# Last stage of a four-layer graph network: a new static order of its steps on the engines

## The chip, the core and the metric

The kernel runs on one core of a Trainium2 chip. The core has five engines that work side by side, each through its own queue in order: TensorE for matmuls (PE; its weight loads are the row PEld), VectorE (DVE), ScalarE (ACT), GpSimd (POOL), and SyncE (SP), which here only issues DMAs. An engine whose next instruction has to wait does nothing else until that wait ends. The metric is the device time of one execution in microseconds (us).

## The reference, cut to what matters

128 graphs of 128 nodes with 128 features pass through four layers; each layer adds its result to `x`. Layers 2 and 3 (counted from 0) are attention layers, and with the end of layer 1 they make up the stage that the change touches.

```python
h = relu(layernorm(x)); x = x + L0(h, adj)      # relations, normalised
h = relu(layernorm(x)); x = x + L1(h, adj)      # pairwise |x_i - x_j| scores, batch norms over all graphs
h = relu(layernorm(x)); x = x + L2(h, adj)      # 4 heads:
    h = (x @ W + b).reshape(B, N, 4, 32)
    e = leaky(e_i[:, :, None] + e_j[:, None, :]);  e = where(adj > 0, e, NEG)
    out = einsum('bijh,bjhd->bihd', softmax(e, axis=2), h)
h = relu(layernorm(x)); x = x + L3(h, adj)      # 1 head, then elu
```

`L1` ends with a batch norm over all graphs, so nothing after it can start before every graph has passed through the pairwise part.

## The kernel before

Graphs are taken in 32 groups of four (`G = 4`, `NG = 32`). The kernel has three stages, one after the other: layer 0 with the pairwise products of layer 1 (lines 264 to 712), the scores and softmax of layer 1 (714 to 1111), and the last stage (1308 to 1570), which does the end of layer 1 and the whole of layers 2 and 3. A fourth path (`last_stage`, 1122) is taken only for inputs out of bounds and doesn't run here.

In the last stage `attention(g)` (line 1319) writes down the work of one group as up to 59 steps. A step has a name, an engine, a cost in us, the steps that it comes after, the PSUM tiles that it takes and gives back, and the function that emits its instructions. In order of dependence one group is:

- `lz`, `lx` (SP): loads of the layer-1 result and of `x`; five groups have both on the chip and need none. `off` (POOL): the mask. `y` (ACT), `yl` (DVE), `po` (PE), `x1` (DVE): end of layer 1.
- layer 2: `mv2` (DVE, moments), `rs2` (POOL, root, lines 228, 229, 1386, 1387), `h2` (ACT, four instructions, line 1392), `pt2` (PE, transposes), `hT2` (ACT), `pr2` (PE, projection), `v2` (DVE), `w12` (POOL, fill), `wr2` (ACT), `sp2` (POOL, the scores split into three bf16 pieces), `pe2` (PE), `left2` (ACT), `right2` (DVE). Then for the four graphs `ps0`, `ps2` (PE, scores of two graphs each), `e0` to `e3` (ACT, two exponentials each, lines 1481 and 1482), `e0m` to `e3m` (DVE), `w0` to `w3` (PE), `o1`, `o3` (DVE, division by the sums), and `x2` (DVE).
- layer 3: the same chain with one head, `mv3`, `rs3`, `h3`, `pt3`, `hT3`, `pr3`, `v3`, `w13`, `wr3` (line 1433), `sp3`, `pe3`, `left3`, `right3`, `ps`, `e`, `em`, `pv` (line 1544), `o` (line 1549), then `ex` (ACT, line 1558), `x3`, `x4` (DVE), and `out` (SP, line 1563).

That is 15 steps on ACT (28 instructions), 15 on PE, 19 on DVE, 7 on POOL, and up to 3 DMAs for each group.

`_planned` (line 78) turns the steps of all groups into one sequence. It is a list scheduler: it keeps the time at which each engine comes free, and repeatedly takes the step that can start earliest. Group number n may not start before `(n - FIRST) * PERIOD`, that is every 12 us from the sixth on. It counts the PSUM tiles (`ONE = 4` single banks, `TWO = 2` double banks) but not the SBUF buffers of `BUFS` (12 for `x`, 6 for `y`, 2 or 3 for most others); those are waited for on the chip, by the instruction that needs the buffer. Its costs are written into the steps, for instance `h` 1.2, `y` 0.75, `pr` 1.0, `w0` 0.95, `e` 1.05. The sequence fixes the order of every engine's queue; when a step starts on the chip is decided by the semaphores.

`split` (1435) writes into one of four `pieces` buffers, chosen by `g % 4`. Earlier stages use another scheduler, `_ordered` (113).

Of the kernel before, what the change touches and what calls it, by code (L numbers as in the profile page):

```python
# [14 lines left out]
OP = mybir.AluOpType  # L15
# [20 lines left out]


ONE, TWO = 4, 2
PERIOD, FIRST, HOP, LANDING = 12, 5, 0.2, 3.0
HOP1 = 0.4  # L40
TINY = 2.0 ** -100
BUFS = {"y": 6, "x": 12, "off": 10, "st": 8, "mv2": 3, "rs2": 3, "nb2": 3, "h": 7, "hT2": 3, "v2": 3, "wr2": 7,
        "left2": 5, "right2": 5, "e0": 2, "e1": 2, "e2": 2, "e3": 2, "sums2": 3, "o2": 2, "mv3": 2, "rs3": 2,
        "nb3": 2, "hT3": 2, "v3": 2, "wr3": 3, "left3": 2, "right3": 2, "e": 2, "sums3": 3, "o3": 3, "ex": 3}


def _bcast(src, n):
# [17 lines left out]
def _staggered(works, gap):  # L65

    flying, turn = [], 0
    while True:
# [4 lines left out]
                return  # L73
        turn += 1
        flying = [w for w in flying if next(w, works) is not works]


def _planned(groups, period, banks):

    free, done = dict.fromkeys(("SP", "Pool", "ACT", "DVE", "PE"), 0.0), {}
    left = {tag: [0.0] * n for tag, n in banks.items()}
    tag = lambda name: "2" if name[0] == "2" else "1"
    waiting = [list(steps) for steps in groups]
    plan = []
    while any(waiting):
        best = None
        for n, steps in enumerate(waiting):
            for i, (name, engine, cost, after, takes, last, work) in enumerate(steps):  # L90
                if any(a not in done for a in after):
                    continue
                start = max([free[engine], (n - FIRST) * period] + [done[a] + HOP for a in after])
                if takes:
                    bank = sorted(left[tag(takes[0])])
                    if len(bank) < len(takes):
                        continue
                    start = max(start, bank[len(takes) - 1])
                if best is None or start < best[0]:
                    best = start, n, i  # L100
        start, n, i = best
        name, engine, cost, after, takes, last, work = waiting[n].pop(i)
        free[engine] = start + cost
        done[name] = start + cost + (LANDING if engine == "SP" else 0)
        for one in takes:
            left[tag(one)].remove(min(left[tag(one)]))
        for one in last:
            left[tag(one)].append(start + cost + HOP)
        plan.append((start, len(plan), work))
    return [work for _, _, work in sorted(plan, key=lambda p: p[:2])]  # L110


def _ordered(steps, limits, hop):
# [21 lines left out]
    while len(plan) < len(steps):  # L135
        best = None
        for engine, names in ready.items():
            could = []
            for name, since in names.items():
                takes = named[name][4]  # L140
                if all(left[tag] for tag in takes):
                    could.append((max([free[engine], since] + [min(left[tag]) for tag in takes]),
                                  named[name][6], name))
            if could:
                first = min(could)[0]
                one = min((c for c in could if c[0] == first), key=lambda c: c[1])
                if best is None or first < best[0]:
                    best = one
        start, _, name = best
        _, engine, cost, _, takes, gives, _, work = named[name]  # L150
        del ready[engine][name]
        free[engine] = start + cost
        done[name] = start + cost + (LANDING if engine == "SP" else 0)
        for tag in takes:
            left[tag].remove(min(left[tag]))
        for tag in gives:
            left[tag].append(start + cost + hop)
        plan.append(work)
        for f in followers.get(name, ()):
            missing[f] -= 1  # L160
            if missing[f] == 0:
                released(f)
    return plan


@with_exitstack
def tile_gnn_stack(ctx: ExitStack, tc: tile.TileContext, a: dict, out: bass.AP):
# [1140 lines left out]
    with tc.If(nc.values_load(bounded, min_val=0, max_val=1) > 0) as cmp, \  # L1308
# [7 lines left out]
                nc.gpsimd.memset(one, 1.0)  # L1316
                pieces[heads].append(one)

        def attention(g):


            t, steps = {}, []

            def step(name, engine, cost, after, work, takes=(), last=()):
                steps.append(((g, name), engine, cost, [(g, n) for n in after], takes, last, work))

            def sb(name, shape, dtype=F32):
                t[name] = p3.tile(shape, dtype, tag=name, bufs=BUFS[name], name=name)
# [23 lines left out]
            def masked():  # L1352
                nc.gpsimd.tensor_scalar(sb("off", [P, G, P], BF16), M8[g], 0.0, None, op0=OP.is_equal)

            step("off", "Pool", 1.5, lx, masked)
            step("y", "ACT", 0.75, () if on_chip else ("lz",), lambda: nc.scalar.activation(
                t["y"], t["y"], AF.Identity, bias=bias2, scale=scale2[:, 0:1]))
            step("yl", "DVE", 0.65, ("y",), lambda: nc.vector.scalar_tensor_tensor(
                t["y"], t["y"], 0.01, t["y"], op0=OP.mult, op1=OP.max))

            def rest():
                po = bank("po")
                for k in range(G):
                    nc.tensor.matmul(po[:, k, :], t["y"][:, k, :], wtyT, start=True, stop=True)

            step("po", "PE", 0.9, ("yl",), rest, takes=("po",))
            step("x1", "DVE", 0.6, ("po",) + lx, lambda: nc.vector.tensor_tensor(t["x"], t["x"], t["po"], OP.add),
                 last=("po",))

            def layer(n, heads, wx, first):  # L1370
# [62 lines left out]
                            nc.scalar.copy(wr[:, 2 * a:2 * a + 2, 0:P], pr[:, a, :, 0:P])  # L1433

                def split():
                    v, to = t[q("v")], pieces[heads][g % len(pieces[heads])]
                    t[q("sides")] = to
                    for p in range(3):

# [18 lines left out]
                def right():  # L1458
# [1 line left out]
                                            t[q("pe")][0:rows, 1:2, :].to_broadcast([rows, 4, P]),  # L1460
                                            own[0:rows, :, None].to_broadcast([rows, 4, P]), OP.mult)

                step(mv, "DVE", 1.05, ("x1",) if first else ("x2",), moments)
                step(rs, "Pool", 1.7, (mv,), root)
                step(q("h"), "ACT", 1.2, (rs,), normed)
                step(q("pt"), "PE", 0.5, (q("h"),), turned, takes=(q("pt"),))
                step(q("hT"), "ACT", 0.52, (q("pt"),), lambda: nc.scalar.copy(sb(q("hT"), [P, G, P]), t[q("pt")]),
                     last=(q("pt"),))
                step(q("pr"), "PE", 1.0, (q("hT"),), projected, takes=("2" + q("pr"),))
                step(q("v"), "DVE", 0.3, (q("pr"),), scores)  # L1470
                step(q("w1"), "Pool", 0.3, (q("h"),), values)
                step(q("wr"), "ACT", 0.65, (q("v"), q("w1")), values2, last=("2" + q("pr"),))
                step(q("sp"), "Pool", 1.2, (q("v"),), split)
                step(q("pe"), "PE", 0.2, (q("sp"),), crossed, takes=(q("pe"),))
                step(q("left"), "ACT", 0.3, (q("pe"),), lambda: nc.scalar.copy(
                    sb(q("left"), [P, P], BF16)[0:rows], t[q("pe")][0:rows, 0, :]))
                step(q("right"), "DVE", 0.6, (q("left"),), right, last=(q("pe"),))

            def exps(ps, e):

# [7 lines left out]
            for k in range(G):  # L1488
# [20 lines left out]
                                         start=True, stop=True)  # L1509

                if k % 2 == 0:
                    step(ps, "PE", 0.8, ("right2", "off"), summed, takes=(ps, f"ps{k + 1}"))
                step(e, "ACT", 1.05, (f"ps{k // 2 * 2}",), lambda ps=ps, e=e: exps(ps, e))
                step(e + "m", "DVE", 0.62, (e,), lambda ps=ps, e=e: higher(ps, e), last=(ps,))
                step(f"w{k}", "PE", 0.95, (e + "m", "wr2") + ((f"w{k - 1}",) if k % 2 else ()), weighed,
                     takes=("2" + pv,) if k % 2 == 0 else ())
                if k % 2:
                    def scaled(k=k, pv=pv):
# [4 lines left out]
                        nc.vector.tensor_tensor(t["o2"][:, k - 1:k + 1, :].rearrange("p k (a b) -> p k a b", a=4),  # L1523
                                                t[pv][:, :, :, 0:32], sums.to_broadcast([P, 2, 4, 32]), OP.mult)

                    step(f"o{k}", "DVE", 0.55, (f"w{k}",) + (("o1",) if k == 3 else ()), scaled, last=("2" + pv,))

            step("x2", "DVE", 0.62, ("o3",), lambda: nc.vector.scalar_tensor_tensor(
                t["x"], t["o2"], -1.0, t["x"], op0=OP.add, op1=OP.add))

            layer(3, 1, w3x, False)
# [14 lines left out]
            def scaled3():  # L1546
# [2 lines left out]
                nc.vector.tensor_tensor(sb("o3", [P, G, P]).rearrange("p (a b) c -> p a b c", a=2),  # L1549
                                        t["pv"][:, :, :, 0:P], sums.to_broadcast([P, 2, 2, P]), OP.mult)  # L1550

            step("ps", "PE", 0.7, ("right3",), summed3, takes=("ps",))
            step("e", "ACT", 1.05, ("ps",), lambda: exps("ps", "e"))
            step("em", "DVE", 0.62, ("e",), lambda: higher("ps", "e"), last=("ps",))
            step("pv", "PE", 1.0, ("em", "wr3"), weighed3, takes=("2pv",))
            step("o", "DVE", 0.75, ("pv",), scaled3, last=("2pv",))

            step("ex", "ACT", 0.52, ("o",), lambda: nc.scalar.activation(sb("ex", [P, G, P]), t["o3"], AF.Exp))
            step("x3", "DVE", 0.62, ("o",), lambda: nc.vector.scalar_tensor_tensor(
                t["x"], t["o3"], 0.0, t["x"], op0=OP.max, op1=OP.add))  # L1560
            step("x4", "DVE", 0.62, ("x3", "ex"), lambda: nc.vector.scalar_tensor_tensor(
                t["x"], t["ex"], 1.0, t["x"], op0=OP.min, op1=OP.add))
            step("out", "SP", 0.4, ("x4",), lambda: nc.sync.dma_start(
                out[g * G:g * G + G].rearrange("b t c -> t b c"), t["x"]))
            return steps

        with tc.manual_schedule():
            groups = [attention(g) for g in sorted(range(NG), key=lambda g: g not in Y)]
            for work in _planned(groups, PERIOD, {"1": ONE, "2": TWO}):
                work()  # L1570


# [40 lines left out]
```

## Time and profile before

| | |
|---|---|
| median of 3 runs | 2754.09 us (2749.94 to 2755.46) |
| the profiled execution's own time | 2756.67 us |
| its span, first to last instruction | 2754.8 us |
| busy over the span: PE, DVE, ACT, POOL | 89%, 90%, 86%, 62% |
| first instruction of the last stage that uses the batch norm (`y` on ACT) | at 2291.34 us |
| last instruction of the last stage on DVE (`x4`) | starts at 2748.94 us |
| last `out` issued, issue to landing | at 2749.7 us, 2.4 us |
| mean granted TensorE clock | 0.974 |

The profile is of one execution. Its rows give, for an engine and a line of the kernel, how many instructions ran, how long one took, and what ended the idle time in front of it. The view by stretches gives busy time of each engine between two moments; the count in brackets is instructions.

### The profile page before, as it was taken

What the parts mean: (1) busy time and instruction counts of PE and PEld (TensorE: products, weight loads), DVE (VectorE), ACT (ScalarE), POOL (GpSimd) and SP (SyncE); (2) the same over time, 40 slices, a digit from 0 to 9 for tenths busy, and PEclk for the clock granted to TensorE, in tenths of its full rate; (3) what the DMA queues carried; (4) which work ended last, traced back from release to release, by engine and by line L of the source; (5) the groups of instructions that cost most, each with busy time, mean ns of one, the idle gap of its engine ahead of it and who ended that gap; (6) DMA issues with size and microseconds to landing.
All of it is one profiled execution on the core that took longest, in us unless ns stands there. A gap on an engine that the chain in (4) does not pass through costs nothing.

```text
span 2754.8 us, 41902 instructions
## 1 busy us (share of the span) xinstructions
PE 2450.1 (89%) x14521; PEld 1183.4 (43%) x14521; DVE 2477.0 (90%) x4738; ACT 2378.7 (86%) x2821; POOL 1699.9 (62%) x1628
## 2 busy tenths in 40 slices
PE   6999999999999999999997888988888987999896
PEld 3333333333333333333332343444444445777775
DVE  6999999999999999999998799888888887899876
ACT  5999999999999999999998777788877866899885
POOL 6999999999999999999985010010011115565642
PEclk8999999999999999999999999999999999999998
DMA  3455555555555555555542999999999971112200
GB/s 113 180 206 201 206 203 204 205 200 203 199 203 199 203 199 203 202 199 208 200 200 92 408 409 395 386 410 410 411 410 407 409 271 35 56 61 66 62 20 25
DMA packets 185426, 611.43 MB, mean 222 GB/s; under 512 B 31987, under 2 KB 99702, under 8 KB 121718
## 3 DMA queue, kind: packets, MB, share of 16 engines
q1 hardware_dynamic: 184768, 608.50, 57.4%
q8 instruction: 118, 1.93, 0.3%
q14 instruction: 102, 0.84, 0.1%
q10 hardware_dynamic: 438, 0.17, 0.0%
HBM read 312.58 MB, written 296.03 MB: 221 GB/s over the span
## 4 chain that ended last, share of the span: by engine, by line
ACT 34%; PE 22%; DVE 19%; issue 11%; DMA 8%; POOL 5%; SPq 0%; ACTq 0%; POOLq 0%; DVEq 0%
ACT d L365 11%; ACT z L341 11%; PE ps L814 5%; PE hp L327 5%; DVE z L857 4%; DVE d L317 3%; DMA z<-hp 3%; DMA rows<-sk 3%; PE hp L330 2%; POOL d L317 2%; PE pk L821 2%; DMA u<-rows 2%; ACT h L1392 2%; ACT o L462 2%; ACT h L503 2%
## 5 line engine op out<-in xcount | busy, mean ns | idle before, releaser
L317 POOL TENSOR_TENSOR d<-xe 128x2048 f32<-128x2048 f32 x256 | 1074.3, 4202 | 68.6 <-PE hp L327 51.3
L327 PE MATMUL hp<-d,w1T 128*64 128x512 f32 x4096 | 997.3, 601 | 105.5 <-ACT z L341 87.9
L365 ACT ACTIVATE d<-d 128x2048 f32<-128x2048 f32 x384 | 735.6, 1936 | 9.5 <-POOL d L317 5.7
L317 DVE TENSOR_TENSOR d<-xe,xp 128x2048 f32<-128x2048 f32 x256 | 579.0, 2262 | 7.2 <-PE hp L327 4.2
L327 PEld LDWEIGHTS hp<-d,w1T 128*64 128x64 f32 x4096 | 286.6, 136 | 621.0 <-issue 463.4
L341 ACT COPY z<-hp 128x1024 f32<-128x1024 f32 x512 | 517.2, 1029 | 37.1 <-PE hp L330 33.9
L905 POOL TENSOR_TENSOR x<-x,bt 128x512 f32<-128x512 f32 x32 | 50.1, 1565 | 669.0 <-DMA x<-x 540.5
L355 DVE BATCH_NORM_STATS2 st<-z 128x6 f32<-128x512 f32 x512 | 348.9, 682 | 43.4 <-ACT z L341 43.2
L356 DVE BATCH_NORM_STATS2 st<-z 128x6 f32<-128x512 f32 (+1 forms) x512 | 328.9, 642 | 0.0
L857 DVE SCALAR_TENSOR_TENSOR z<-z 128x2048 f32<-128x2048 f32 x128 | 299.4, 2339 | 7.9 <-ACT z L839 7.9
L839 ACT ACTIVATE z<-z,bias,scale 128x2048 f32<-128x2048 f32 x128 | 267.1, 2087 | 10.1 <-DVE bias L751 7.9
L843 ACT ACTIVATE zr<-z,bias,scale 128x2048 f32<-128x2048 f32 x128 | 267.3, 2088 | 0.9 <-DMA z<-hp 0.9
L330 PE MATMUL hp<-both_t,xw 128*64 128x512 f32 x1024 | 267.8, 594 | 0.0
L814 PE MATMUL ps<-z,w2z 128*32 128x512 f32 x1024 | 142.6, 629 | 61.2 <-DVE z L857 60.5
L821 PEld LDWEIGHTS pk<-pick,su 128*128 128x128 f32 x1024 | 125.8, 193 | 145.6 <-DVE su L835 107.1
L821 PE MATMUL pk<-pick,su 128*128 128x16 f32 x1024 | 138.3, 267 | 31.6 <-DVE su L835 31.0
L1508 PE MATMUL pv<-wr,e 128*128 128x128 f32 x1024 | 140.3, 283 | 5.8 <-DVE e L1485 4.0
L330 PEld LDWEIGHTS hp<-both_t,xw 128*64 128x64 f32 x1024 | 81.3, 138 | 140.0 <-issue 140.0
L814 PE MATMUL ps<-zr,w2r 128*32 128x512 f32 x1024 | 140.3, 620 | 0.0
L814 PE MATMUL ps<-z,w2l 128*32 128x512 f32 x1024 | 139.6, 614 | 0.0
L1508 PEld LDWEIGHTS pv<-wr,e 128*128 128x128 f32 x1024 | 128.3, 196 | 13.7 <-DVE e L1485 4.4
L1485 DVE SCALAR_TENSOR_TENSOR e<-e,ps 128x512 f32<-128x512 f32 x160 | 106.5, 676 | 26.6 <-ACT ps L1482 25.8
(241 smaller groups left out, 3798.0 us busy)
## 6 DMA issues: line engine op xcount, KB each, us to landing
hp<-z SPq DMA_DIRECT2D x248, 1024.0 KB, 3.9
z<-hp SPq DMA_DIRECT2D x248, 1024.0 KB, 13.2
x<-x SPq DMA_DIRECT2D x118, 256.0 KB, 6.0
u<-rows SPq DMA_DIRECT2D x32, 384.0 KB, 11.6
x<-in_x_dram SPq DMA_DIRECT2D x32, 256.0 KB, 5.6
adj<-in_adj_dram SPq DMA_DIRECT2D x32, 256.0 KB, 5.8
out_dram<-x SPq DMA_DIRECT2D x32, 256.0 KB, 2.4
z<-y SPq DMA_DIRECT2D x27, 256.0 KB, 11.9
```

The source lines that it names most:

```text
L317: eng.tensor_tensor(d, ahead, x[:, None, None, :].to_broadcast([P, 2, KC, P]), OP.max if t == BY_MAX else OP.subtract)
L327: nc.tensor.matmul(hp[64 * hh:64 * hh + 64, c:c + 512], w1T2 if by_max else w1T, d[:, hh, c:c + 512], start=True, stop=not by_max, skip_gr ...
L330: nc.tensor.matmul(hp[64 * hh:64 * hh + 64, c:c + 512], XW[i // NT // 2][:, i // NT % 2, :], both_t.rearrange("p h k i -> p h (k i)")[:, h ...
L341: nc.scalar.copy(half_of(b, t), linear.pop(i))
L355: nc.vector.bn_stats(st[:, 2 * t, :], hs[:, 0:512])
L356: nc.vector.bn_stats(st[:, 2 * t + 1, :], hs[:, 512:1024 - P * last])
L365: nc.scalar.activation(diffs[i], diffs[i], AF.Abs)
L814: nc.tensor.matmul(ps[32 * c:32 * c + 32, :], w[:, w0:w0 + 32], v[:, 512 * c:512 * c + 512], start=j0 == 0, stop=w is w2r, skip_group_chec ...
L821: nc.tensor.matmul(pk[:, kk, 0:16], su[:, kk, :], pick.rearrange("p h j -> p (h j)"), start=True, stop=True)
L843: nc.scalar.activation(zr, z1, AF.Relu, bias=bias1, scale=scale1[:, 0:1])
L857: nc.vector.scalar_tensor_tensor(z0, z0, 0.01, z0, op0=OP.mult, op1=OP.max)
L1508: nc.tensor.matmul(t[pv][:, k % 2, hd, :], t[e][:, hd, :], flat[:, at:at + P], start=True, stop=True)
```

## The change

`_planned` is replaced by `_ranked`, and the steps get new costs, ranks and joining times. No instruction is added, removed or altered; the index of the `pieces` buffer changes from the group's number to its place in the turn.

```diff
-PERIOD, FIRST, HOP, LANDING = 12, 5, 0.2, 3.0
+LANDING = 3.0
 HOP1 = 0.4
+HOPS, DEEP, ARRIVING, NEAR = 0.1, 0.25, 2.4, 0.025
+LATE = {"SP": 0.0, "Pool": 0.02, "ACT": 0.1, "DVE": 0.08, "PE": 0.1}
+LANDED = {"load": 6.0, "out": 5.0, "out0": 5.0}
+TILES = (("y", "lz", "po"), ("x", "lx", "out"), ("off", "off", "ps0 ps2 ps"), ("mv2", "mv2", "rs2"), ("rs2", "rs2", "h2"),
...
+EVERY = 16.7
+RANK3 = {"off": 260, "y": 228, "yl": 425, "po": 78, "x1": -85, "mv2": 311, "rs2": 127, "h2": 106, "pt2": -67,
...
+         "pv": -160, "o": -8, "ex": 360, "x3": 119, "x4": 187, "out": 299, "lz": 146, "lx": -73}
+JOIN3 = (20, 2, 0, 0, 1, 2, 28, 29, 0, 13, 49, 23, 67, 94, 51, 151,
+         131, 78, 137, 199, 221, 127, 166, 143, 241, 183, 223, 276, 237, 165, 178, 294)
-def _planned(groups, period, banks):
...
+def _ranked(steps, limits, held, hop, within=0.0):
+    named, place = {q[0]: q for q in steps}, {q[0]: n for n, q in enumerate(steps)}
+    free, done, left = dict.fromkeys(LATE, 0.0), {}, {tag: [0.0] * n for tag, n in limits.items()}
+    needs, reads, open_ = {}, {}, []
+    for tag, at, readers in held:
+        if at in named:
+            of = needs.setdefault(at, {})
+            of[tag] = of.get(tag, 0) + 1
+            for r in readers:
+                reads.setdefault(r, []).append(len(open_))
+            open_.append([tag, len(readers), 0.0])
...
+    while len(plan) < len(steps):
+        best = None
+        for engine, names in ready.items():
+            could = []
+            for name in names:
+                start = max(free[engine], since[name])
+                for tag, n in needs.get(name, {}).items():
+                    start = max(start, sorted(left[tag])[n - 1] if len(left[tag]) >= n else 1e9)
+                could.append((start, named[name][4], place[name], name))
+            if could and (best is None or min(could)[0] < best[0]):
+                first = min(could)[0]
+                best = (first,) + min((c for c in could if c[0] <= first + within), key=lambda c: c[1:3])
...
+        free[engine], done[name] = round(start + cost - LATE[engine], 2), round(start + cost, 2)
+        if engine == "SP":
+            done[name] += LANDED.get(name[0], LANDING if isinstance(name[0], str) else ARRIVING)
...
-        def attention(g):
+        def attention(n_th, g, fourth):
...
-                steps.append(((g, name), engine, cost, [(g, n) for n in after], takes, last, work))
+                after = [n if isinstance(n, tuple) else (g, n) for n in after]
+                steps.append(((g, name), engine, cost, after, EVERY * n_th + RANK3[name], JOIN3[n_th], work))
...
-            step("y", "ACT", 0.75, () if on_chip else ("lz",), lambda: nc.scalar.activation(
+            step("y", "ACT", 0.81, () if on_chip else ("lz",), lambda: nc.scalar.activation(
...
-                    v, to = t[q("v")], pieces[heads][g % len(pieces[heads])]
+                    v, to = t[q("v")], pieces[heads][n_th % len(pieces[heads])]
...
-                step(q("h"), "ACT", 1.2, (rs,), normed)
+                step(q("h"), "ACT", 1.65, (rs,), normed)
...
-                step(q("pr"), "PE", 1.0, (q("hT"),), projected, takes=("2" + q("pr"),))
+                step(q("pr"), "PE", 1.50 if first else 1.15, (q("hT"),), projected, takes=("2" + q("pr"),))
...
-                step(q("sp"), "Pool", 1.2, (q("v"),), split)
+                step(q("sp"), "Pool", 1.25, (q("v"),) + ((fourth, q("pe")),) * (fourth is not None), split)
...
-            groups = [attention(g) for g in sorted(range(NG), key=lambda g: g not in Y)]
-            for work in _planned(groups, PERIOD, {"1": ONE, "2": TWO}):
+            held, turns = [], sorted(range(NG), key=lambda g: g not in Y)
+            steps = [one for n, g in enumerate(turns) for one in attention(n, g, turns[n - 4] if n > 3 else None)]
+            have = {one[0] for one in steps}
+            held += [(tag, (g, at), [(g, r) for r in readers.split()]) for g in turns for tag, at, readers in TILES
+                     if (g, at) in have]
+            for work in _ranked(steps, {"one": ONE, "two": TWO} | BUFS, held, HOPS):
                 work()
```

What `_ranked` does differently:

- It counts the SBUF buffers too (`TILES` names the step that fills each and the steps that read it), so a step that would wait for a buffer on the chip is put later in the plan.
- Each engine first asks which of its steps could start earliest; among those that could start at the same moment it takes the one with the lowest rank, `EVERY * n_th + RANK3[name]`, where `n_th` is the group's place in the turn.
- A group's steps may begin at `JOIN3[n_th]` us instead of at every 12th us. The joining times don't rise steadily with the place, so groups change places.
- An engine is taken as free `LATE` before its step's result is there (0.1 us on ACT and PE).
- The costs are longer: on ACT `h` 1.65 instead of 1.2, the pair of exponentials 1.19 instead of 1.05; on PE `pr2` 1.50 instead of 1.0, `w0` 1.09 instead of 0.95; on DVE `mv` 1.26 instead of 1.05; on POOL `rs` 1.85 instead of 1.7.

## Prediction

> **What bounds the kernel now.** I read four views, in this order. First the busy time by stretch, for the last stage cut in three: the ramp (from the first `y` to the time when ACT is first kept busy), the body, and the drain.
>
> ```profile
> core 0: us, PE busy (x) PEld busy (x) DVE busy (x) ACT busy (x) POOL busy (x), PEclk, DMA share, GB/s
> 2291.30:2312.00 20.70, 15.06 (x94) 12.61 (x94) 16.44 (x67) 13.81 (x30) 19.00 (x41) 0.84 0.11 41
> 2312.00:2720.00 408.00, 370.78 (x2735) 294.85 (x2733) 347.56 (x1113) 356.39 (x840) 227.74 (x652) 0.97 0.15 46
> 2720.00:2754.80 34.80, 16.45 (x85) 12.56 (x85) 16.30 (x38) 12.40 (x29) 5.28 (x20) 0.67 0.12 34
> ```
>
> The stage lasts 463.5 us. ACT works for 382.6 of them, DVE for 380.3, PE for 402.3 by its rows. So three engines need nearly the same time, and no one of them is full: in the body ACT idles 408 - 356.4 = 51.6 us, PE 37, DVE 60. The drain is half empty on all. The other two stages have the same instructions in the same order in both programs (laid side by side, the orders first differ behind the first `y` and `off`), so what changes lies in these 463.5 us.
>
> Is PE the bound, as its 402 says? The Trainium skill warns against this reading (Perfetto Trace Analysis, Identifying the Most-Contended Engine): matmul busy time is not a good measure, because matmuls are pipelined. The trace bears it out: in a dense stretch `po` is followed by the next group of matmuls after 0.90 us, though its eight records span 1.05. With start-to-start times read so (po 0.9, pt 0.49, pr 1.45 and 0.92, pe 0.22, ps pair 0.8, w 0.89 each, ps 0.65, pv 0.92) a group takes 11.4 us of PE, and 32 groups 365. By the rows PE would be the floor with 402, and little over 40 us could go; by the pitch ACT is, with 383. I take the pitch.
>
> Second, who ends ACT's waits in the body:
>
> ```profile
> ACT h L1392 <- POOL nb L1387: 10.4, 16, 1.9
> ACT ex L1558 <- DVE o L1549: 7.2, 7, 2.2
> ACT h L1392 <- POOL wr L1424: 6.6, 5, 2.2
> ACT e L1481 <- PE ps L1498: 5.5, 6, 2.0
> ACT wr L1433 <- DVE v L1415: 5.0, 4, 2.1
> ACT left L1475 <- PE pe L1453: 4.8, 9, 1.4
> ACT e L1481 <- PE ps L1538: 3.7, 4, 1.3
> ```
>
> (us in total, times, longest.) No wait repeats in every group, and none is long. They are the mark of a queue whose next step was put too close behind the step that it follows from. Loads are no part of it: `y` waits 0.4 us for a DMA once.
>
> Third, the chain that ended last, in the drain (start, us, what):
>
> ```profile
> 2735.50 2.10 PE pr L1407 x8
> ...
> 2742.06 0.58 PE ps L1535
> 2742.64 0.55 PE ps L1538 x4
> ...
> 2745.07 2.10 PE pv L1544 x8
> ```
>
> Here group 31 is alone, step after step, on a slow PE: its last `x2` starts at 2727.55 and its last `x4` ends at 2749.63, 22 us of pure latency. In dense stretches `pv` takes 1.1, not 2.1.
>
> Fourth, the orders of both programs on each engine, without times.
>
> **The change, part by part.** Nothing is added or removed on any engine: 480 steps on PE, 480 on ACT, 608 on DVE, 224 on POOL and 86 DMAs in both. So engine work stays, and the sum is one of gaps.
>
> *The body.* I counted, for each dependency that leaves an engine and comes back to it, how much of that engine's own work stands between the two steps in its queue, and set it against what the way round takes. Example: ACT's `e` to its `ex` goes over `em` 0.68, `pv` 1.22 and `o` 0.88, with four hand-overs of 0.1 (the chain shows 0.02 to 0.09 each): 3.2 us. Before, group 16 has one step between them, `17.h3` with 1.56, so 1.6 us must be idled unless something else was late; after, it has eight. The median of all groups goes from 5 steps between to 11. Of 27 such ways round, for the 29 groups that are not the last three to join:
>
> | engine | too short before | too short after |
> |---|---|---|
> | ACT | 19 times, 11.9 us | 2 times, 0.2 us |
> | PE | 16 times, 10.3 us | 4 times, 4.9 us |
> | DVE | 16 times, 6.0 us | 9 times, 7.0 us |
> | together | 28.2 us | 12.1 us |
>
> POOL's way from `rs3` to `sp3`, 4.4 us round, was too short in 13 of all 32 groups by 25.9 us, and is in 8 by 11.9; this feeds the 17 us of `h` behind `nb` and `wr`, though a step on POOL itself costs nothing there. More groups are under way: a group stays for 128 DVE steps from `x1` to `x4` before and 151 after, 6.7 and 7.9 groups at once. The count explains why it got better, but not all of the 51.6 us: lateness is passed on. I assume that idle time falls as the count does, to 12.1 / 28.2 = 0.43: 51.6 to 22, **29 us** off. Bounds: at least the 12 us of ACT's own short ways (11.9 - 0.2) would go; at most ACT runs as in its best 20 us of this trace (19.90 busy from 2310 to 2330), so 356.4 / 0.99 = 360, 48 off. I take 29 because then ACT is at 94% of the body, as it is in the best longer stretches of this profile (23.8 of 25 us from 2450 on, 95%); nothing here shows more over a long time.
>
> *The drain.* The way of group 31 from `x2` on stays as it is, 22 us. But more work of the others is left to lie beside it: after `31.e3` ACT has 14.3 us of steps instead of 8.9, DVE after `31.x2` 13.7 instead of 10.0, PE after `31.w3` 10.0 instead of 5.9. What moves in there was in the body: **4 us** off (3.7 to 5.4). It is bounded at 2 the other way if these steps stand in front of group 31's: `25.ps`, `24.pv` and `25.pv` do, 2.5 together.
>
> *The ramp.* POOL has five `off` ahead of the first root, instead of four: 1.5 us each, so the first `h` starts about 1.5 us later than at 2300.13. Then five roots follow without a `w12` between them, and the second `h` doesn't wait (1.85 before). **1 us** lost, between 2 lost and 2 won.
>
> *Loads.* SP's queue now holds `lx` and `lz` of a group apart, and `out` of one group stands ahead of `lx` of another. A load that waits for a buffer also holds the outs behind it, for which nobody waits but the next load. From the last `out` ahead of it (`x4` on DVE) to `x1` of the loaded group DVE has at least 26 steps before, but 11 for group 22 and 15 for group 15 after. The way is `out` 0.4 and two more issues, then 3.3 to land: 4.5 us, or 7 if the buffer is that of this very `out`, which has to land first (2.4); 11 steps of 0.62 are 6.8. So it just fits, and I cost it at nothing; with that cover gone it is the rival on the other side.
>
> *Buffers and pieces.* The plan counts them now, so their waits are in the orders above. The price of a wrong guess is the same as for loads. `pieces` by place: the writer comes four groups later, and no wait of `sp` on `pe` is visible before; nothing, at most 1 us.
>
> *A rule against it.* The costs are fixed numbers, but the Trainium skill (SBUF — State Buffer, section SBUF: two separate sides) says that VectorE and GpSimd exclude each other on one pair of ports, for the whole instruction, where DVE reads two inputs from SBUF and GpSimd reads SBUF too. A denser plan would meet this more often. In this trace `rs` on line 229 has a minimum of 1.04 us, a mean of 1.07 and a maximum of 1.52; over the four POOL instructions of a root the means lie above the minima by 0.2 us. By the rule, each root could be held by a 0.69 us DVE instruction, 64 x 0.69 = 44 us of lateness; by the rows it is 64 x 0.2 = 13, which the before kernel pays too, off its path. I take the rows: nothing.
>
> Sum: 29 + 4 - 1 = 32 us. The profiled execution's 2756.7 becomes 2724.7; against the median of three, 2.6 lower, **2722**.
>
> **Rivals.**
> 1. *Saturation.* The plan's durations are this trace's, so the chip follows it and ACT runs at 99%: 48 + 5 = 53 off, 2701; a softer form at 97% (356.4 / 0.97 = 367) gives 41 + 5, 2708. For it: ACT held 99% for 40 us from 2310. Against: DVE's short ways don't fall, and three engines would have to be full at once. 0.17.
> 2. *Moved waits.* ACT's own short ways go and the lateness of `h` stays, since POOL and DVE still come late: 12 to 18 off, 2736 to 2742. For it: DVE's row in the table. 0.17.
> 3. *Loads late: slower.* The order was made for one timing; where `out` comes later than planned, the load behind it in SP's queue is late, and `x1` stands at the head of DVE's queue while everything behind it waits. 16 loads follow an `out`. It takes 2 us at each to eat 32 us; at 2.5 each the time is 2762. For it: 11 and 15 steps where there were 26. Against: only two are so close, and DVE's own delay moves `x4` and `x1` alike. 0.07.
> 4. *No effect.* Gaps close in one place and open in another, within 5 us: 2754. 0.05.
>
> The likeliest, 2712 to 2733, has 0.54. The two ends of its unknown costs are 12 + 2 - 2 and 48 + 5 + 2 off; the range for 8 in 10 runs from 2706 to 2744, leaving out the hardest saturation and the slower cases. Before's runs lie within 0.2% of each other (5.5 us), so that is what can be told from no change: faster by more 0.88, within 0.05, slower by more 0.07.
>
> **What would show it.** Right: the stage from the first `y` to the last `x4` takes some 425 us instead of 458; ACT's idle time in the body is near 22 us, `ex` behind `o` and `wr` behind `v` nearly gone from its waits; granted clock in the body at 1.0; the drain some 22 us after the last `x2`, with more instructions in it. Wrong: `x1` or `y` behind a DMA for several us (rival 3), or `h` behind POOL for 17 us as before (rival 2).

## The result and the profile after

The changed kernel takes **2717.9 us** (median of 4 runs, 2716.38 to 2719.59) against 2754.3 for the kernel before on the same chip: a ratio of 0.9871, 95% interval 0.9854 to 0.9888. That is 36.4 us less; 32 were forecast. The profiled execution took 2717.82 us with a span of 2716.0 and a mean clock of 0.98.

Busy time by stretch of the changed kernel, with the last stage cut as in the prediction (ramp, body, drain):

```profile
core 0: us, PE busy (x) PEld busy (x) DVE busy (x) ACT busy (x) POOL busy (x), PEclk, DMA share, GB/s
2289.20:2309.90 20.70, 13.97 (x89) 12.83 (x90) 15.47 (x64) 13.96 (x30) 18.76 (x39) 0.79 0.29 99
2309.90:2681.20 371.30, 353.10 (x2694) 280.07 (x2693) 340.14 (x1095) 349.40 (x830) 232.08 (x648) 1.00 0.15 47
2681.20:2716.00 34.80, 21.68 (x135) 16.85 (x133) 21.64 (x58) 16.36 (x39) 7.02 (x25) 0.73 0.15 41
```

The stage went from 463.5 to 426.8 us, and all of the 36.7 is in the body, since ramp and drain are cut at fixed lengths. ACT's idle time in the body went from 51.6 to 371.3 - 349.4 = 21.9 us. The stretch that drains has 135 matmul records where it had 85, and 39 ACT instructions where it had 29.

The waits of ACT in the body of the changed kernel (us in total, times, longest):

```profile
ACT h L1442 <- POOL nb L1437: 7.8, 11, 1.3
ACT left L1525 <- PE pe L1503: 2.7, 5, 0.8
ACT h L1442 <- POOL wr L1474: 2.4, 4, 1.1
ACT wr L1483 <- DVE v L1465: 2.2, 2, 1.2
ACT e L1531 <- PE ps L1588: 1.3, 3, 0.7
...
ACT ex L1608 <- DVE o L1599: 0.7, 2, 0.4
...
ACT e L1531 <- PE ps L1548: 0.6, 2, 0.3
```

Every line of the list in the prediction is shorter, and the longest single wait of ACT is 1.3 us where it was 2.3. `ex` behind `o` is down from 7.2 to 0.7. `h` behind POOL is down from 17.0 to 10.2, though POOL has the same work. `wr` behind `v`, which was to be nearly gone, still waits 3.4 us (5.6 before). No engine waits for a load of `y` or `x`.

The end of the chain that ended last (start, us, what), in the drain of the changed kernel:

```profile
2701.25 2.06 PE pv L1594 x8
2703.31 0.53 PE ps L1585
2703.85 0.55 PE ps L1588 x4
...
2706.28 2.10 PE pv L1594 x8
...
2710.15 0.69 DVE x L1611
```

Group 31 still ends alone on a slow PE, `pv` at 2.1 us. From its last `x2` at 2688.28 to the end of the last `x4` it takes 22.6 us; 22.1 before. From the first `y` to the end of the last `x4` the stage takes 421.6 us instead of 458.3; the prediction had 425.

### The profile page after: what moved, and what is told of

Same layout as the page of the kernel before. It is cut to its first block, busy times and chain, and to the rows that moved or that the text cites. A ratio compares the mean times of both kernels' runs of the same rounds, so it can differ in the third digit from the quotient of the medians.

```text
span 2716.0 us, 41908 instructions
## 1 busy us (share of the span) xinstructions
PE 2431.7 (90%) x14521; PEld 1169.3 (43%) x14521; DVE 2477.9 (91%) x4738; ACT 2375.6 (87%) x2821; POOL 1690.9 (62%) x1628
## 4 chain that ended last, share of the span: by engine, by line
ACT 33%; PE 21%; DVE 19%; issue 11%; DMA 10%; POOL 6%; SPq 0%; ACTq 0%; POOLq 0%; DVEq 0%
ACT z L385 11%; ACT d L409 11%; PE hp L371 5%; PE ps L858 4%; DMA rows<-sk 4%; DVE z L901 3%; DMA z<-hp 3%; DVE d L361 3%; DMA u<-rows 3%; PE hp L374 2%; POOL d L361 2%; ACT o L506 2%; PE pk L865 2%; ACT h L547 2%; ACT hn L506 1%
## 5 line engine op out<-in xcount | busy, mean ns | idle before, releaser
L1558 PE MATMUL pv<-wr,e 128*128 128x128 f32 x1024 | 134.0, 278 | 2.0 <-ACT wr L1483 1.1
L1442 ACT ACTIVATE h<-x,nb,rs 128x128 f32<-128x128 f32 x256 | 105.5, 489 | 20.6 <-POOL nb L1437 17.8
```

## The experiments

A "way" in the expectations is a dependency that leaves an engine and comes back to it; it is too short when that engine's own work between the two steps is less than the way round takes. "The stage" runs from the first `y` to the end of the span. The table is read with the sections below; the last column was worked out when all runs were known and is explained at the end.

| kernel | time, us | ratio to before, 95% | stage, us | ACT idle in the body | queues replayed, us |
|---|---|---|---|---|---|
| before | 2754.3 | | 463.5 | 51.6 | 465.6 |
| after | 2717.9 | 0.9871 (0.9854 to 0.9888) | 426.8 | 21.9 | 426.5 |
| no ranks | 2772.1 | 1.0079 (1.0057 to 1.0100) | 478.9 | 66.4 | 466.3 |
| even joins | 2739.0 | 0.9950 (0.9929 to 0.9971) | 445.3 | 35.8 | 438.7 |
| neither | 2773.1 | 1.0076 (1.0059 to 1.0093) | 477.3 | 63.0 | 473.9 |
| old costs | 2738.5 | 0.9946 (0.9929 to 0.9962) | 446.4 | 33.2 | 457.1 |
| `h` at 1.67 | 2739.4 | 0.9947 (0.9932 to 0.9962) | 449.7 | 41.0 | 440.9 |
| ranks / 4 | 2752.2 | 0.9985 (0.9978 to 0.9993) | 460.1 | 46.3 | 450.3 |
| neither, old costs | 2767.2 | 1.0045 (1.0029 to 1.0061) | 477.3 | 63.2 | 477.2 |
| `ex` later | 2792.4 | 1.0133 (1.0115 to 1.0150) | 500.0 | 86.0 | 496.3 |
| `ex`, `x4` later | 2760.6 | 1.0022 (1.0014 to 1.0029) | 468.8 | 58.7 | 470.8 |
| fifth `off` later | 2718.0 | 0.9867 (0.9849 to 0.9884) | 426.1 | 21.4 | 427.0 |
| tables anew | 2724.3 | 0.9888 (0.9874 to 0.9902) | 428.7 | 24.1 | 428.2 |
| tables searched on | 2721.6 | 0.9876 (0.9861 to 0.9891) | 428.8 | 22.7 | 424.9 |

Idle time and stage length each come from the kernel's one profiled execution. The kernel before, run beside each, had medians of 2753.5 to 2756.0 us, and the ratios are to those.

### Which part of the change does it: ranks, joins, or neither

No ranks, from the changed kernel:

```diff
-                steps.append(((g, name), engine, cost, after, EVERY * n_th + RANK3[name], JOIN3[n_th], work))
+                steps.append(((g, name), engine, cost, after, EVERY * n_th, JOIN3[n_th], work))
```

> The ranks of the kinds are taken out of the new planner; its durations, buffers and joining times stay. Theory (ways round): idle time in the body follows the sum by which ways round in the queues are too short. That sum is 28.0 us in the order before (51.6 us idle on ACT in the body) and 14.8 after (21.9 idle), so 1.5 to 1.8 us idle for each. Here it is 52.9, so 79 to 97 us idle: 2775 to 2793 us, slower than before. Rival A (durations: true costs and counted buffers make the gain, ranks hardly matter): 2718 to 2726. Rival B (joining times, more groups at once): 2718 to 2726 too, since they are kept.

Even joins, that is a group every 12 us as before:

```diff
-                steps.append(((g, name), engine, cost, after, EVERY * n_th + RANK3[name], JOIN3[n_th], work))
+                steps.append(((g, name), engine, cost, after, EVERY * n_th + RANK3[name], max(0.0, 12.0 * (n_th - 5)), work))
```

> The joining times are those of before (every 12 us from the sixth group); ranks, durations and buffers are the new ones. Ways round: sum too short 11.1 against 14.8 us in the changed kernel, 15.8 us of other groups' ACT steps in the drain against 14.3: 2711 to 2719. Rival A: 2718 to 2722. Rival B (the table of joining times makes the gain): 2735 to 2750.

Neither, both edits together, which leaves the traced durations and the counted buffers alone:

> Neither ranks nor the table of joining times: a list scheduler with the trace's durations and counted buffers. Ways round: sum too short 59.6, so 89 to 107 us idle: 2785 to 2805, slower than before. Rival A (durations and buffers): 2718 to 2730. Rival B: 2735 to 2750.

Measured: 2772.1, 2739.0 and 2773.1. Without ranks the planner does worse than the one it replaced, whatever the joins. With the ranks and even joins, some 14 of the 36 us are left. So the durations and the counted buffers, taken alone, bring no gain; with them the kernel is 20 us slower than before. The waits of ACT in the body, first without ranks:

```profile
ACT h L1442 <- POOL nb L1437: 17.1, 24, 1.9
ACT e L1531 <- PE ps L1548: 12.0, 13, 2.1
ACT hT L1517 <- PE pt L1448: 10.8, 11, 2.3
```

and with even joins:

```profile
ACT h L1442 <- POOL nb L1437: 10.5, 19, 1.1
ACT left L1525 <- PE pe L1503: 7.6, 10, 1.8
ACT e L1531 <- PE ps L1548: 6.8, 9, 2.0
```

`h` behind POOL and `e` behind the scores (`ps`, line 1548) stand in both lists; the third line differs. In the changed kernel they are 7.8 and 0.6 us. None of these is a load. For no ranks and for the kernel with neither, the count of short ways had the direction right and the size too large, by 3 and 12 us at least. For even joins it was wrong: it forecast 2711 to 2719, since by the count that order is better than the changed kernel (11.1 us too short against 14.8), and 2739.0 was measured.

### Are the durations needed? And how much hangs on the tables?

Old costs: the changed kernel, with every cost in `attention` set back to what it was, for instance

```diff
-                step(q("h"), "ACT", 1.65, (rs,), normed)
+                step(q("h"), "ACT", 1.2, (rs,), normed)
...
-                step(q("pr"), "PE", 1.50 if first else 1.15, (q("hT"),), projected, takes=("2" + q("pr"),))
+                step(q("pr"), "PE", 1.0, (q("hT"),), projected, takes=("2" + q("pr"),))
```

> The new planner with its ranks, joining times and buffers, but with the step costs of before. Ways round: sum too short 23.9, so 36 to 43 us idle, and 19.5 us of ACT steps in the drain against 14.3: 2728 to 2738. Rival A (durations): 2745 to 2754, most of the gain lost. Rival B: 2718 to 2722.

Next, a single cost, changed by 1%. It changes the planning alone, not the work:

```diff
-                step(q("h"), "ACT", 1.65, (rs,), normed)
+                step(q("h"), "ACT", 1.67, (rs,), normed)
```

> The changed kernel with one planning cost altered by 1%: h 1.67 instead of 1.65. Ranks and joining times stay. 1644 of 1878 places of the sequence change. If the gain is in the kinds' ranks and the true durations as such: 2717 to 2721. If the tables only fit the one sequence for which they were chosen: ways with under 1 us to spare rise from 107 to 155, at 0.21 to 0.30 us each 10 to 14 us more idle: 2728 to 2734.

Ranks at a quarter, which keeps their order among the steps of one group but lets a group come before the next one sooner:

```diff
-                steps.append(((g, name), engine, cost, after, EVERY * n_th + RANK3[name], JOIN3[n_th], work))
+                steps.append(((g, name), engine, cost, after, EVERY * n_th + RANK3[name] / 4, JOIN3[n_th], work))
```

> The changed kernel with the ranks of the kinds at a quarter of their size, so that a group's place counts for more against the kind. Ways with under 1 us to spare: 170 (107 in the changed kernel, 262 without ranks), 13 to 19 us more idle: 2731 to 2738. Rival (only the sign of the ranks matters, they break ties): 2718 to 2722. Rival (ranks must outweigh the groups' places, else they do nothing): near 2772, as without ranks.

And neither ranks nor joins with the old costs:

> No ranks, joins every 12 us, counted buffers, and the step costs of before: the new planner brought as near to the old one as its parameters allow. Ways with under 1 us to spare: 272 (228 before, 306 with the trace's costs), at 0.21 to 0.27 us each 57 to 73 us idle: 2759 to 2776. Rival (the old costs were what made the old order better than the plain new one): as before, 2750 to 2758. Rival (costs don't matter without ranks): 2770 to 2776.

Measured: 2738.5, 2739.4, 2752.2 and 2767.2. Changing `h` by 0.02 us costs as much as setting all costs back: 21 us. In that order 401 of ACT's 480 steps stand at another place than in the changed kernel's. Its waits (ACT, body, `h` at 1.67):

```profile
ACT h L1442 <- POOL nb L1437: 9.4, 12, 1.7
ACT e L1531 <- PE ps L1548: 8.0, 12, 1.3
ACT left L1525 <- PE pe L1503: 6.5, 9, 1.2
```

All three are longer than in the changed kernel; `e` behind the scores grew most, from 0.6 to 8.0 us. So the last 21 us belong to one sequence, and the tables name it only together with these durations. The tables are not worthless under others: with the old costs they take 28.7 us off (2767.2 to 2738.5), and with `h` at 1.67 the kernel is still 34 us below the one with neither. Accurate costs by themselves are worth nothing: without ranks and joins, the old costs give 2767.2 and the traced ones 2773.1. That planner is still slower than the one before by 12 us; which of its other traits (counted buffers, a hand-over of 0.1 instead of 0.2, engines free early) costs them was not tried.

Of the four forecasts by short ways, the last was met. Old costs came out just over the upper end of theirs, `h` at 1.67 at least 5 us over, and ranks at a quarter at least 14 us over. Neither rival fits the ranks at a quarter: their size matters, and not just their sign.

### Can a short way be mended by hand?

The kernel before, with each `ex` moved behind five more of ACT's steps, so that it no longer waits for `o`; its `x4` and `out` stay just behind it:

```diff
+LATER = 5
...
+    for g in [name[0] for _, name, _ in plan if name[1] == "ex"]:
+        at = lambda step: next(i for i, p in enumerate(plan) if p[1] == (g, step))
+        i = at("ex")
+        acts = [n for n in range(i + 1, len(plan)) if plan[n][2] == "ACT"]
...
+        to = acts[LATER - 1]
+        moved = plan.pop(i)
+        plan.insert(to, moved)
+        for step in ("x4", "out"):
+            i = at(step)
+            if i < to:
+                plan.insert(to, plan.pop(i))
```

> The order before, with one thing done by hand: each ex on ACT is put five ACT steps later in the queue (its x4 and out follow it). Ways round: the wait of ex behind o in the body, 7.2 us before, falls to 0 to 2 us. Ways with under 1 us to spare fall from 228 to 207; the kernels so far idled 0.21 to 0.30 us of ACT in the body for each such way, so 4 to 6 us of the idle time go: 2747 to 2750 us. Rival (gaps close in one place and open in another): the wait goes, the idle time stays at 51 us, 2752 to 2756.

It took 2792.4 us, 36 more than before, which neither theory had. The waits of DVE in the body say why; first the kernel before, then the edited one:

```profile
DVE e L1485 <- ACT ps L1482: 20.7, 30, 2.9
...
DVE x L1561 <- ACT ex L1558: 1.6, 3, 1.1
```

```profile
DVE x L1576 <- ACT ex L1573: 37.8, 25, 4.5
DVE e L1500 <- ACT ps L1497: 18.4, 26, 2.9
```

`x4` on DVE comes right behind `ex`, and now it stands at the head of DVE's queue 25 times until `ex` is done: 36 us more than before, and the stage is 36.5 us longer. A step put too close behind the one it follows cost, in this order, nearly its whole wait. So the next kernel also moves `x4`, five steps of DVE behind `ex`:

```diff
+        for step, engine, n in (("x4", "DVE", 5), ("out", "SP", 0)):
...
+            after = at("ex" if step == "x4" else "x4")
+            behind = [k for k in range(after + 1, len(plan)) if plan[k][2] == engine]
+            plan.insert(max(i, behind[n - 1] + 1 if n and len(behind) >= n else after + 1), moved)
```

> Like the kernel with ex put five ACT steps later in the old order, but x4 is put five DVE steps behind it as well, so that DVE doesn't stand in front of x4 while ex is still to come (that wait was 37.8 us there, 1.6 in the order before). Ways round: x4 behind ex below 4 us, ex behind o below 2 us; the 36 us lost there come back, and the ways of ex that were too short go: 2746 to 2753. Rival (any step put later holds its buffers longer, and that is what cost 36 us): 2780 or more.

2760.6, over the forecast by 8 us and far from its rival: the 36 us are back but for 5, so they were DVE's blocked queue and not a buffer kept longer. But the 7.2 us of `ex` that were in the list before were not won. ACT's waits in the body of this kernel:

```profile
ACT h L1409 <- POOL nb L1404: 16.4, 17, 2.0
ACT h L1409 <- POOL wr L1441: 7.9, 7, 2.3
ACT e L1498 <- PE ps L1515: 7.7, 7, 2.1
ACT wr L1450 <- DVE v L1432: 7.3, 7, 2.0
```

`ex` is gone from the list, and `h` behind POOL is up from 17.0 to 24.3. The gap was closed in one place and opened in others. Here a listed wait was no gain that could be had by removing it alone.

### The ramp

The changed kernel with the fifth `off` put behind two roots on POOL:

```diff
+    pools = [i for i, p in enumerate(plan) if named[p[1]][1] == "Pool"]
+    offs = [i for i in pools if plan[i][1][1] == "off"]
+    roots = [i for i in pools if plan[i][1][1] == "rs2"]
+    plan.insert(roots[1], plan.pop(offs[4]))
```

> The changed kernel, with the fifth off on POOL put behind the first two roots; nothing else moves. Ramp: the first h starts 8.7 us after the first y instead of 10.2. If the ramp counts in full, 1.5 us off: 2715 to 2717. Rival (what is won at the start is lost in the body, where ACT waits for others): first h earlier, time 2717 to 2719.

2718.0, the same, as the rival had it. The first `h` starts 9.71 us after the first `y` instead of 10.23: only half a microsecond of the 1.5 comes back, as the root then waits for its moments.

### Other tables, and a better sequence

If the tables are only a name for one good sequence, unrelated values found against the same planner should do as well. Both kernels are the changed one with other numbers in `RANK3` and `JOIN3`. They were found by random steps that keep what lowers the end of the planner's own plan: one began from ranks of zero and even joins, the other from the change's tables.

```diff
-RANK3 = {"off": 260, "y": 228, "yl": 425, "po": 78, "x1": -85, "mv2": 311, "rs2": 127, "h2": 106, "pt2": -67,
+RANK3 = {"off": 2260, "y": 1623, "yl": 1539, "po": 7, "x1": 545, "mv2": 497, "rs2": 1344, "h2": 2684, "pt2": -1188,
...
-JOIN3 = (20, 2, 0, 0, 1, 2, 28, 29, 0, 13, 49, 23, 67, 94, 51, 151,
+JOIN3 = (0, 0, 0, 0, 0, 3, 0, 26, 36, 12, 61, 79, 87, 103, 105, 112, 132, 131, 149, 182, 180, 194, 207, 217,
...
```

> The changed kernel with other tables: ranks all at zero and joins every 12 us were the start, and random steps were kept where the planner's own end time (the largest planned end of a step) came earlier; the ranks that came out have nothing in common with those of the change. Planned end against measured stage so far: 426.5 and 426.8 us (changed kernel), 438.8 and 445.3 (even joins), 441.4 and 449.7 (h 1.67), 450.3 and 460.1 (quarter ranks), 466.3 and 478.9 (no ranks), 474.0 and 477.3 (neither). Here the planned end is 428.2. Theory (the gain is what a search against true durations and counted buffers finds, whatever the ranks): stage 429 to 438, 2720 to 2730. Rival (the ranks of the change know which kinds have to come first; others don't do): 2735 or more.

> The changed kernel with its tables searched on by random steps: planned end 424.9 instead of 426.5. If the planner's end is met as in the changed kernel: 2716 to 2717. If that close fit is an accident of the one sequence and others run 3 to 12 us over their plan: 2720 to 2728.

2724.3 and 2721.6. Ranks that have nothing in common with the change's (the joining times rise alike) reach 85% of its gain (30.8 of 36.4 us), as forecast. The second plan ends 1.6 us before the change's, yet its stage is 2 us longer in the one profile of each: an end planned that much earlier was not met. The intervals of both ratios overlap that of the changed kernel, so these times do not clearly tell the three apart. No version here beat the changed kernel.

### All orders replayed

The last column of the table replays each kernel's queues as they stand: every engine takes its steps in order, each starting when its engine, its inputs and its buffers are there. Durations, hand-overs, buffers and the turn of the `pieces` are the change's for all of them, so the order of the queues is the only thing that differs. The replay ends with the last `out` landed. It misses the measured stage by 4.7 us in the mean of the 14 kernels: it is 0.3 us short for the changed kernel and 2.1 long for before, and at worst 12.6 short (no ranks) and 10.7 long (old costs). The 0.3 flatters it: the measured stage goes on for 2.7 us behind the last landing in both programs, and up to that landing the replay is 2.4 us too long for the changed kernel and 4.8 for before. It gives the difference of before and after as 39.1 us, where 36.7 were measured. It has the two orders mended by hand right to 4 us (496.3 and 470.8 for 500.0 and 468.8), and 12 of the 18.5 us that even joins lose.

Two things were tried in the replay alone, so they are worked out and not shown on the chip. With unlimited SBUF buffers neither order changes its length, with unlimited PSUM before ends 4.2 us sooner and after 0.5. With each single step made longer or shorter by up to 5% at random, the changed order ends at 426.2 to 428.9. (With all steps of a kind drawn alike it ends at 423 to 433, as the sums of work then change too.) So the 21 us of `h` at 1.67 are, by the replay, those of another sequence, and not of a sequence that a small delay upsets; replayed in the order of the change, that `h` costs 0.65.

Not tried on the chip: an order planned without counting SBUF buffers, because its queues, replayed with the buffers there are, wait on each other for ever.

## Why the prediction was right, and where it was not

The mechanism is as forecast: the same instructions, with less time at the heads of the queues. How much less was in part a lucky guess, as said below. The measured stage against the sum 29 + 4 - 1, with the terms read from ACT's busy time in the three stretches:

| term | forecast | measured |
|---|---|---|
| ACT's idle time in the body | 29 | 29.7 (51.6 to 21.9) |
| ACT's work moved into the drain | 4 | 4.0 (12.40 to 16.36) |
| ramp | -1 | +0.1 (13.81 to 13.96 of ACT's work in it) |
| ACT's busy time as a whole | 0 | 2.9 (382.6 to 379.7) |
| together | 32 | 36.7 |

**What was mis-sized: "engine work stays".** The work does, but not the time that it covers. ACT's mean durations are the same in both (the pair of exponentials 594 and 597 ns before, 597 and 599 after). In the changed kernel they stand closer (timeline of ACT, in a dense stretch):

```profile
2482.78 0.58 ACT L1531 ACTIVATE e<-ps 128x512 f32<-128x512 f32 x1
2483.26 0.57 ACT L1532 ACTIVATE ps<-ps 128x512 f32<-128x512 f32 x1
2483.78 0.79 ACT L1406 ACTIVATE y<-y,bias,scale 128x512 f32<-128x512 f32 x1
2484.48 0.57 ACT L1531 ACTIVATE e<-ps 128x512 f32<-128x512 f32 x1
```

An instruction of 0.58 is followed by the next after 0.48, and the overlap counts once. Counts times mean durations give some 465 us of ACT's instructions in both stages, so the 2.9 us are more overlap and not shorter work. They are 2.9 of the 4.7 by which the sum fell short.

**The ramp** was the smaller miss. The first `h` starts 10.23 us after the first `y`, 1.44 later than before, as costed; ACT's timeline then has

```profile
2299.46 1.65 ACT L1442 ACTIVATE h<-x,nb,rs 128x128 f32<-128x128 f32 x4 [5.90 <-POOL nb L1437]
2301.50 1.65 ACT L1442 ACTIVATE h<-x,nb,rs 128x128 f32<-128x128 f32 x4 [0.39 <-POOL nb L1437]
```

and the second `h` waits 0.39 instead of 1.85, which gives it all back.

**What was right by luck: the 0.43.** The count of short ways was taken as a factor for all idle time. On this pair it gave 22 and 21.9 was measured. But the count of the first experiments has 14.8 and 28.0 us for the same two orders, a factor of 0.53, which would have taken 24 off instead of 29. And it says that DVE's short ways do not fall (6.0 to 7.0), while DVE's idle time in the body fell from 60.4 to 31.2; its largest wait, 20.7 us before, is now

```profile
DVE e L1535 <- ACT ps L1532: 8.4, 14, 1.5
```

On even joins the same way of counting failed by at least 20 us. Its later form (ways with under 1 us to spare) failed on ranks at a quarter by 14, on `ex` later by 42, and on its repair it was at least 7 us too low. It leaves out that a late step makes other queues late, and that a gap closed in one place opens in another. (POOL's way from `rs3` to `sp3`, given as 4.4 us, also lacks its six hand-overs of 0.1; it did not enter the sum.) What stands in its place is the replay of all queues, which needs the traced durations, hand-overs, buffers and both orders. It could have been made before the run.

**PE's rows are no floor.** Their 402 us were not one: PE's busy time in the stage is 388.8 after, with the same work. That the pitch's 365 is the right figure is not shown. Granted clock in the body rose from 0.97 to 1.00, as forecast.

**The rivals.** Saturation (2701 to 2708) did not come: ACT reaches 99.5% only for 50 us, in these two stretches, and idles elsewhere:

```profile
2475.00:2500.00 25.00, 24.61 (x193) 19.74 (x191) 24.17 (x77) 24.92 (x61) 15.89 (x47) 1.00 0.24 75
2500.00:2525.00 25.00, 24.51 (x195) 20.35 (x194) 23.36 (x77) 24.83 (x58) 14.29 (x37) 1.00 0.18 54
```

Moved waits (2736 to 2742) is wrong for the changed kernel, where `h` behind POOL fell. Late loads came halfway: SP's queue now waits for an `out` to land before it can load, which it did not before,

```profile
SPq L1392 <- DMA out_dram<-x: 23.2, 14, 2.8
```

but no engine waits for these loads, so the cover just fits, as costed. No effect is ruled out. **Ports:** the root's second POOL instruction takes 1.07 us in the mean before and after, at most 1.52 and 1.60; the denser order costs it nothing, as the rows said. Some other POOL instructions did grow (`off` from 1.53 to 1.59 us), and POOL's busy time in the stage with them, from 252.0 to 257.9; why was not tested.

**Open.** Why three orders ran 9 to 13 us over their replay and one 11 under, when the changed kernel is within 0.3, or 2.4 by the last landing. The profiled execution after also began the stage 2.1 us sooner than before's, in stages that are the same in both; that is no effect of the change, and it is not in the stage's 36.7.

## What to carry to other kernels

When only the order of in-order queues changes, replay both orders whole, with traced durations and every wait (here right to 4.7 us in the mean, 12.6 at worst); a count of tight places, or the list of waits, ranks orders roughly and misjudges repairs. A planner's tables are worth what its whole plan is worth: search them against the planned end, and search again when any duration changes, since 1% on one cost gave back 21 of 36 us here. Before moving one step later, look at who stands in line for it: moving `ex` ended its own 7 us of waits, put 36 on DVE, and left ACT idle for 34 us more.

## What the hardware showed unasked

The granted TensorE clock in the body follows, roughly, how full the queues are: 1.00 in the four orders where ACT idles 21 to 24 us, 0.98 to 0.99 where it idles 33 to 46, 0.96 to 0.98 from 52 to 66, and 0.94 at 86 (`ex` later), whose body in the view by stretches is

```profile
2308.90:2753.40 444.50, 385.65 (x2737) 304.21 (x2735) 350.59 (x1115) 358.47 (x842) 225.58 (x656) 0.94 0.14 43
```

Here PE's rows cover 385.65 us with 2737 matmul records, where the changed kernel's body has 353.10 with 2694. How much of that is the clock was not taken apart. Whether a loose order pays a second time on PE is therefore not shown: the replay, which knows no clock, accounts for this stage without it to within 3.7 us.
